# Parting joined results on VectorE instead of GpSimd, in four pieces of two operations

## The chip, the cores and the metric

The kernel runs on one core of one Trainium2 chip. The metric is device time in microseconds, from one launch to its end. The core has five engines, each with an instruction queue that it works through in order: TensorE (PE, with its weight loads as PEld), VectorE (DVE), ScalarE (ACT), GpSimd (POOL) and SyncE (SP). In this kernel SP issues all DMA transfers.

## The reference, cut to what matters

The input x has four images of 64 channels of 256x256, in fp32. Four layers follow each other. Layers 0, 2 and 3 are long convolutions with a filter for each channel (here done as products with Toeplitz matrices, along columns and rows, and a residual `x * bias`). Layer 1 goes to a Haar basis, mixes the channels twice, shrinks, adds up, and goes back:

```
f1 = haar2d(x)
acc = 0
for i in range(2):
    f3 = f1 * v[i]
    f4 = einsum('bchw,oc->bohw', f3, conv_w[i])
    acc += sign(f4) * relu(abs(f4) - tau[i])
x = haar2d(acc, inverse=True) + x
```

`haar2d` adds and subtracts neighbours, scaled by the square root of one half, over eight levels along the rows and then the columns.

## The kernel before, in words

The work is cut in three phases, each over two groups of two images (GROUPS, NB). Phase A does layer 0 and the forward Haar transform and writes coefficients (`coef`) to HBM. Phase B mixes the channels of one group and writes the results (`mixed`, and for the last group's raw second products `unshrunk`). Phase C reads them, does the inverse transform and layers 2 and 3, and writes the output.

Each phase is a list of small pieces of code. `beside` interleaves two lists by hand: phase B of group 0 lies beside the second half of phase A, phase B of group 1 beside the first part of phase C. The order in which the pieces issue is the order on every engine's queue, since the schedule is written out by hand; tiles come from pools, in rings with a fixed number of buffers by tag.

Phase B runs over 64 steps s of two units u = 2s and 2s+1 (one for each `v[i]`, `conv_w[i]`). Each unit has three pieces j = 0, 1, 2. The operations of a unit and the lines under which the profile shows them before the change:

- `mix`, TensorE, L651: eight products of 64x512 into PSUM tile f (tile ft is the input).
- `multiply`, VectorE, L670: x = f * v, into a tile of ring "x", which has two buffers. In group 1, odd units from step 2 on are raw: L667 copies the product out instead, and nothing else is done with it here.
- `sign` and `magnitude`, ScalarE, L676 and L685. Sign fills a tile of ring "m", which has three buffers. In group 0 the magnitude goes to PSUM, in group 1 in place into the x tile.
- `less` and `threshold`, VectorE, L690 and L695: subtract tau, then max with 0 and multiply by the sign.
- `exchange`, ScalarE, L701, a copy named other.
- `add`, GpSimd, L713 and L714 (even units, which start a tile of ring "gt", three buffers) and L710 (odd units).
- `store`, SP, L719: gt goes to `mixed`.
- `load_v` (L603 and L605: v and its thresholds) and `load_f` (L592: ft), SP.

Steps 0 and 1 need something more, since the rows of the coarsest Haar levels lie in their tiles. `join` (VectorE, L623 to L630) does the last level before mixing, once for each image, on 64 partitions and 256 elements at a time. `part` (GpSimd, L636 to L643) undoes it on the results gt of steps 0 and 1, on 64 partitions and 512 elements (both images). Both take a spare tile through the helper `four`. `part` is called in the piece u = 6, j = 0, right after `add(4)`, and the stores of steps 0 and 1 come right after it.

What else lies around: phase A's forward transform on GpSimd (L388, L390), its evictions of PSUM on ScalarE (L488) and VectorE (L508, L521); phase C's inverse transform on GpSimd (L429, tiles i and at the end ci), the product c0ps on TensorE (L352) that takes ci, the Toeplitz products c1r, c1c, c2r, c2c (L340), their evictions on ScalarE (L897 z, L909 ch) and VectorE (L928 cy and o), the scaling of loaded coefficients g on ScalarE (L406), and on SP the loads toep (L163), g (L806) and x (L150) and the stores of raw results (L727), of coef (L525) and of the output (L937).

Of the kernel before, what the change touches and what calls it, by code (L numbers as in the profile page):

```python
# [41 lines left out]
F32 = mybir.dt.float32  # L42
AF = mybir.ActivationFunctionType
ALU = mybir.AluOpType
# [3 lines left out]
P = 128  # L48
# [20 lines left out]
NB = B // GROUPS  # L69
# [14 lines left out]
W = 2 * N  # L84
# [16 lines left out]
def conv_haar_kernel(  # L101
    ctx: ExitStack, tc: tile.TileContext, x, zT, w1, wbd, cols, wo, decay, wo_first, decay_first, bias, forward, inverse, pack, v, tau, per_level, v_rows, out
):
    nc = tc.nc
# [16 lines left out]
    def pool(name, bufs, stack=ctx, **kw):  # L121
        return stack.enter_context(tc.tile_pool(name=name, bufs=bufs, reuse_waits="tile", **kw))
# [173 lines left out]
    def half(r):  # L296
        return slice(r * ROW, (r + 1) * ROW)
# [150 lines left out]
    def run(ops, count):  # L448
        for _ in range(count):
            next(ops, None)  # L450
# [117 lines left out]
    def phase_b(grp):  # L568
# [4 lines left out]
        def raw(u):  # L573
            return grp == GROUPS - 1 and u % 2 == 1 and FULL <= u // 2 < STEPS
# [4 lines left out]
        def step_of(ap, s, images):  # L579

            n = NB * W
            at = ap.offset + s // 2 * PAIR + s % 2 * P // CI * n
            rows = bass.AP(ap.tensor, at, [[n, P // CI], [STEPS // 2 * PAIR, CI], [1, n]])
            return rows, images.rearrange("p b w -> p (b w)")

        def load_f(s):
            if s >= STEPS:
                return
            d = st[s]
            d["f"] = bp.tile([P, NB, W], F32, tag="ft", name=f"ft_{grp}_{s}", bufs=4)  # L590
            rows, f = step_of(coef[grp], s, d["f"])
            nc.sync.dma_start(f, rows)  # L592
# [17 lines left out]
            if grp == GROUPS - 1 and not raw(2 * s + 1):  # L610
                fetch(1, 1, "raw")

        def four(name, at, b):

            tiles = [st[s][name] for s in range(2)]
            tiles.append(bp.tile([P, NB, W], F32, tag="m", name=f"spare_{name}_{grp}_{b}", bufs=3))
            return [t[at, b, bass.ts(h, N)] for t in tiles for h in range(2)]

        def join(image):

            a, b, c, d, t, u = four("f", half(image), image)
            op = nc.vector.tensor_tensor
            op(t, a, b, ALU.add)  # L623
            op(b, a, b, ALU.subtract)
            op(u, c, d, ALU.add)
            op(d, c, d, ALU.subtract)
            nc.vector.tensor_scalar(c, b, math.sqrt(2.0), None, ALU.mult)
            nc.vector.tensor_scalar(d, d, math.sqrt(2.0), None, ALU.mult)
            op(a, t, u, ALU.add)
            op(b, t, u, ALU.subtract)  # L630

        def part():

            a, b, c, d, t, u = four("g", half(0), slice(0, NB))
            op = nc.gpsimd.tensor_tensor
            op(t, a, b, ALU.add)  # L636
            op(b, a, b, ALU.subtract)
            nc.gpsimd.tensor_scalar(u, c, math.sqrt(2.0), None, ALU.mult)
            op(a, t, u, ALU.add)
            nc.gpsimd.tensor_scalar(d, d, math.sqrt(2.0), None, ALU.mult)  # L640
            op(c, b, d, ALU.add)
            op(d, b, d, ALU.subtract)
            op(b, t, u, ALU.subtract)  # L643

        def mix(u):
            s, i = divmod(u, 2)
            un[u]["f4"] = bps.tile([P, NB, W], F32, tag="f4", name=f"f4_{grp}_{u}", bufs=1)
            for b in range(NB):
                for r in range(2):
                    q = r ^ b  # L650
                    nc.tensor.matmul(  # L651
                        un[u]["f4"][half(q), b, :],
                        mixers[0][half(r), bass.ts(i, C)],
                        st[s]["f"][half(r), b],
                        start=True,
                        stop=True,
                        tile_position=(r * ROW, q * ROW),
                    )
# [5 lines left out]
        def multiply(u):  # L664
            if raw(u):
                t = st[u // 2]["raw"] = bp.tile([P, NB, W], F32, tag="raw", name=f"raw_{grp}_{u}", bufs=3)
                nc.vector.tensor_copy(t, un[u]["f4"])  # L667
                return
            un[u]["x"] = bp.tile([P, NB, W], F32, tag="x", name=f"x_{grp}_{u}", bufs=2)
            nc.vector.tensor_tensor(un[u]["x"], un[u]["f4"], both(u, "v"), ALU.mult)  # L670

        def sign(u):
            if raw(u):
                return
            un[u]["m"] = bp.tile([P, NB, W], F32, tag="m", name=f"m_{grp}_{u}", bufs=3)
            nc.scalar.activation(un[u]["m"], un[u]["x"], AF.Sign)  # L676

        def magnitude(u):
            if raw(u):
                return  # L680
            if grp == GROUPS - 1:
                un[u]["a"] = un[u]["x"]
            else:
                un[u]["a"] = bps.tile([P, NB, W], F32, tag="a", name=f"a_{grp}_{u}", bufs=1)
            nc.scalar.activation(un[u]["a"], un[u]["x"], AF.Abs)  # L685

        def less(u):
            if raw(u):
                return
            nc.vector.tensor_tensor(un[u]["a"], un[u]["a"], both(u, "tau"), ALU.subtract)  # L690

        def threshold(u):
            if raw(u):
                return
            nc.vector.scalar_tensor_tensor(un[u]["m"], un[u]["a"], 0.0, un[u]["m"], ALU.max, ALU.mult)  # L695

        def exchange(s):

            st[s]["other"] = bp.tile([P, W], F32, tag="other", name=f"other_{grp}_{s}", bufs=2)
            for q in range(2):  # L700
                nc.scalar.copy(st[s]["other"][half(q)], st[s]["f"][half(1 - q), 1])  # L701

        def add(u):
            s, i = divmod(u, 2)
            if raw(u):
                un[u].clear()
                return
            m = un[u]["m"]
            if i:
                nc.gpsimd.tensor_tensor(st[s]["g"], st[s]["g"], m, ALU.add)  # L710
            else:
                g = st[s]["g"] = bp.tile([P, NB, W], F32, tag="gt", name=f"gt_{grp}_{s}", bufs=3)
                nc.gpsimd.tensor_tensor(g[:, 0], m[:, 0], st[s]["f"][:, 0], ALU.add)  # L713
                nc.gpsimd.tensor_tensor(g[:, 1], m[:, 1], st[s]["other"], ALU.add)  # L714
            un[u].clear()

        def store(s):
            to, g = step_of(mixed[grp], s, st[s]["g"])
            nc.sync.dma_start(to, g)  # L719
            st[s].clear()  # L720

        def store_raw(s):
            if s < FULL:
                t = st[s]["raw"] = bp.tile([P, NB, W], F32, tag="raw", name=f"none_{grp}_{s}", bufs=3)
                nc.gpsimd.memset(t, 0.0)
            to, g = step_of(unshrunk, s, st[s]["raw"])
            nc.sync.dma_start(to, g)  # L727

        def piece(u, j):

            s, i = divmod(u, 2)
            if j == 0:
                if u < units:
                    multiply(u)
                if 0 < u <= units and grp == GROUPS - 1:
                    less(u - 1)
                if 1 < u <= units + 1:
                    add(u - 2)
                if i == 0 and s == 3:
                    part()  # L740
                    store(0)
                    store(1)
                if i == 0 and s > 3 and not raw(2 * s - 3):
                    store(s - 2)
                if i and raw(2 * s - 1):
                    store(s - 1)
            elif j == 1:
                if 0 < u <= units and grp < GROUPS - 1:
                    less(u - 1)
                if u + 1 < units and grp < GROUPS - 1:  # L750
                    mix(u + 1)
                if u < units:
                    sign(u)
                if i and s < STEPS and grp == GROUPS - 1:
                    store_raw(s)
                if 0 < u <= units:
                    threshold(u - 1)
                if i == 0 and s > 0:

                    load_v(s + 2)  # L760
                    if grp < GROUPS - 1:
                        load_f(s + 3)
            else:
                if u + 1 < units and grp == GROUPS - 1:
                    mix(u + 1)
                if i and s > 0 and grp == GROUPS - 1:
                    load_f(s + 3)
                if u < units:
                    magnitude(u)
                if i == 0 and s < STEPS:  # L770
                    exchange(s)

        def start():
            mixers.append(bp.tile([P, P], F32, tag="mix", name=f"mix_{grp}", bufs=1))
# [257 lines left out]
    bp = pool("b", 2, during)  # L1032
# [4 lines left out]
    a = a[-2 * A_PIECES :]  # L1037
# [7 lines left out]
    bp = pool("b2", 2, during)  # L1045
# [132 lines left out]
```

## Time and profile before

| | us |
|---|---|
| median of 3 runs (lowest to highest) | 2484.69 (2483.29 to 2487.93) |
| profiled execution, its own time | 2485.05 |
| its span, first to last instruction | 2483.2 |
| mean granted TensorE clock | 0.984 of full |
| busy: PE, PEld | 2261.3, 1863.9 |
| busy: DVE, ACT, POOL | 1775.6, 1392.2, 2080.2 |
| `part` in group 0, group 1 (start of first to end of last) | 456.83 to 467.7, 1132.1 to 1144.0 |

The busy times are averages over stages with different limits: phase B of group 0 runs from about 420 to 1000 of the span, that of group 1 from about 1090 to 1790, and the rest of phase C alone until the end. A line of the timeline or the chain begins with its time in us from the span's start.

### The profile page before, as it was taken

The page shows a single profiled execution, that of the slowest core. Times are in us where ns is not written, and L with a number is a line of the kernel's source. Part 1 is how long each engine was busy: PE and PEld are TensorE (multiplying, and loading weights), DVE is VectorE, ACT ScalarE, POOL GpSimd, SP SyncE. Part 2 cuts the span into 40 slices and gives each one's busy share as a digit, 9 for nine tenths or more (in the row PEclk, how much of TensorE's full clock was granted, in tenths as well). Part 3 has the DMA queues.
Part 4 walks back from the last instruction along what each step waited for, and adds up shares of the span by engine and source line. Part 5 has one row for each costly group of instructions (what it writes and reads, how often), then busy time and mean ns, then how long its engine had stood idle before and what let it go on. Part 6 is the DMA issues. An engine that isn't in the chain of part 4 may idle for free.

```text
span 2483.2 us, 119306 instructions
## 1 busy us (share of the span) xinstructions
PE 2261.3 (91%) x53298; PEld 1863.9 (75%) x53298; DVE 1775.6 (72%) x1943; ACT 1392.2 (56%) x2318; POOL 2080.2 (84%) x2428
## 2 busy tenths in 40 slices
PE   6999999777777777777999999999899999999999
PEld 5788887444444444555887887888899999999998
DVE  4533335799999999766777778777577777777763
ACT  1322233677777777255666766667555655565652
POOL 2988887999999999778776878778879999999990
PEclk9999999899999999988999999999999999999999
DMA  6788887699999999657998999999866666666643
GB/s 184 246 281 302 300 297 300 246 372 347 359 346 357 357 339 353 211 188 261 328 325 310 342 331 321 334 324 337 280 204 219 211 220 216 218 213 213 220 161 109
DMA packets 222968, 688.03 MB, mean 277 GB/s; under 512 B 31470, under 2 KB 32815, under 8 KB 218232
## 3 DMA queue, kind: packets, MB, share of 16 engines
q1 hardware_dynamic: 222456, 680.40, 78.1%
q8 instruction: 419, 6.86, 1.1%
q14 instruction: 93, 0.76, 0.1%
HBM read 428.16 MB, written 252.12 MB: 274 GB/s over the span
## 4 chain that ended last, share of the span: by engine, by line
PE 47%; DMA 2%; DVE 2%; issue 1%; POOL 1%; ACT 1%; SPq 0%; DVEq 0%; ACTq 0%; POOLq 0%
PE c2c L340 10%; PE c2r L340 10%; PE c1c L340 10%; PE c1r L340 9%; PE c0ps L352 4%; PE f L651 4%; DMA g<-mixed 1%; DMA toep<-filt 1%; DVE cy L928 0%; POOL i L429 0%; DVE x L670 0%; DMA unshrunk<-raw 0%; DVE x L690 0%; ACT ch L909 0%; DMA out<-o 0%
## 5 line engine op out<-in xcount | busy, mean ns | idle before, releaser
L429 POOL TENSOR_TENSOR i<-i,g 128x16 f32<-128x16 f32 x744 | 441.5, 615 | 27.2
L651 PE MATMUL f<-ft,mix 64*64 64x512 f32 x2048 | 302.8, 614 | 117.6 <-DVE x L670 104.0
L340 PEld LDWEIGHTS a2ps<-toep,ay 64*64 64x64 f32 x8192 | 298.4, 136 | 122.7 <-DVE f L521 50.8
L340 PE MATMUL a2ps<-toep,ay 64*64 64x128 f32 (+3 forms) x8192 | 336.5, 303 | 23.2 <-DVE f L521 18.1
L340 PEld LDWEIGHTS c1c<-toep,ch 64*64 64x64 f32 x8192 | 311.8, 133 | 43.8 <-issue 14.0
L340 PEld LDWEIGHTS c2c<-toep,ch 64*64 64x64 f32 x8192 | 304.8, 134 | 51.1 <-issue 12.8
L340 PEld LDWEIGHTS a1ps<-toep,x 64*64 64x64 f32 x8192 | 279.2, 134 | 65.6 <-issue 39.0
L340 PE MATMUL c1c<-toep,ch 64*64 64x128 f32 (+3 forms) x8192 | 317.2, 297 | 7.9 <-issue 4.6
L340 PE MATMUL c2c<-toep,ch 64*64 64x128 f32 (+3 forms) x8192 | 314.7, 298 | 8.5 <-ACT ch L909 7.5
L340 PE MATMUL c1r<-toep,z 64*64 64x192 f32 (+3 forms) x8192 | 317.0, 298 | 5.3 <-issue 3.2
L340 PEld LDWEIGHTS c1r<-toep,z 64*64 64x64 f32 x8192 | 298.3, 134 | 29.5 <-issue 11.9
L340 PE MATMUL a1ps<-toep,x 64*64 64x256 f32 (+3 forms) x8192 | 314.0, 299 | 6.7 <-issue 3.8
L340 PEld LDWEIGHTS c2r<-toep,cy 64*64 64x64 f32 x8192 | 298.5, 134 | 27.2 <-issue 12.5
L340 PE MATMUL c2r<-toep,cy 64*64 64x128 f32 (+3 forms) x8192 | 316.3, 298 | 2.9 <-issue 2.6
L429 POOL TENSOR_TENSOR ci<-i,g 128x1024 f32<-128x1024 f32 x124 | 313.9, 2553 | 4.5
L676 ACT ACTIVATE m<-x 128x1024 f32<-128x1024 f32 x194 | 205.9, 1061 | 158.5 <-DVE x L670 107.5
L488 ACT COPY ay<-a1ps 128x512 f32<-128x512 f32 x256 | 137.5, 589 | 272.6 <-PE a1ps L340 272.0
L713 POOL TENSOR_TENSOR gt<-m,ft 128x512 f32<-128x512 f32 x128 | 163.8, 1279 | 143.4 <-DVE m L695 136.2
L909 ACT COPY ch<-c2r 128x512 f32<-128x512 f32 x256 | 137.1, 589 | 259.7 <-PE c2r L340 259.4
L670 DVE TENSOR_TENSOR x<-f,v 128x1024 f32<-128x1024 f32 x192 | 233.4, 1216 | 29.6 <-PE f L651 26.4
L508 DVE SCALAR_TENSOR_TENSOR x<-x,bias_sb,a2ps 128x512 f32<-128x512 f32 x256 | 179.5, 742 | 94.6 <-PE a2ps L340 43.2
L909 ACT COPY ch<-c1r 128x512 f32<-128x512 f32 x256 | 137.5, 594 | 169.2 <-PE c1r L340 168.8
(86 smaller groups left out, 3983.9 us busy)
## 6 DMA issues: line engine op xcount, KB each, us to landing
toep<-filt SPq DMA_DIRECT2D x768, 112.0 KB
ft<-coef SPq DMA_DIRECT2D x128, 512.0 KB
mixed<-gt SPq DMA_DIRECT2D x128, 512.0 KB
g<-mixed SPq DMA_DIRECT2D x256, 256.0 KB
x<-in_x SPq DMA_DIRECT2D x128, 256.0 KB
coef<-f SPq DMA_DIRECT2D x128, 256.0 KB
x<-in_x SPq DMA_DIRECT2D x32, 1024.0 KB
v<-in_v SPq DMA_DIRECT2D x64, 512.0 KB
```

What stands on the lines that cost most here:

```text
L340: nc.tensor.matmul(ps[r][half(c), j % 2, k * ROW :], data[half(r), c, k, bass.ts(j, ROW)], t(r, c)[:, : N - k * ROW], start=k == 0, stop=k ...
L352: nc.tensor.matmul(ps[r][half(c)].rearrange("p h k -> p (h k)"), matrix[half(r)], pairs(r, c).rearrange("p h k -> p (h k)"), start=True, s ...
L429: engine.tensor_tensor(to, s, d, op)
L488: later(lambda y=y, ps=ps: nc.scalar.copy(y, ps))
L508: nc.vector.scalar_tensor_tensor(to, old, bias_sb[:, c : c + 1], ps, ALU.mult, ALU.add)
L651: nc.tensor.matmul(un[u]["f4"][half(q), b, :], mixers[0][half(r), bass.ts(i, C)], st[s]["f"][half(r), b], start=True, stop=True, tile_posi ...
L670: nc.vector.tensor_tensor(un[u]["x"], un[u]["f4"], both(u, "v"), ALU.mult)
L676: nc.scalar.activation(un[u]["m"], un[u]["x"], AF.Sign)
L713: nc.gpsimd.tensor_tensor(g[:, 0], m[:, 0], st[s]["f"][:, 0], ALU.add)
L909: later(lambda y=y, ps=ps: nc.scalar.copy(y, ps))
```

## The change

`part` moves from GpSimd to VectorE. It becomes a generator that gives up after each of its eight operations, and four pieces run two of them each: at the ends of the pieces (u, j) = (6, 2), (7, 0), (7, 1) and (7, 2), in both groups. The stores of steps 0 and 1 move from the piece (6, 0) to the end of the piece (7, 2). The spare tile comes from ring "x" (two buffers) instead of ring "m" (three); `join` keeps ring "m".

```diff
-        def four(name, at, b):
+        def four(name, at, b, tag, bufs):
             tiles = [st[s][name] for s in range(2)]
-            tiles.append(bp.tile([P, NB, W], F32, tag="m", name=f"spare_{name}_{grp}_{b}", bufs=3))
+            tiles.append(bp.tile([P, NB, W], F32, tag=tag, name=f"spare_{name}_{grp}_{b}", bufs=bufs))
             return [t[at, b, bass.ts(h, N)] for t in tiles for h in range(2)]
...
-            a, b, c, d, t, u = four("f", half(image), image)
+            a, b, c, d, t, u = four("f", half(image), image, "m", 3)
...
         def part():
-            a, b, c, d, t, u = four("g", half(0), slice(0, NB))
-            op = nc.gpsimd.tensor_tensor
-            op(t, a, b, ALU.add)
-            op(b, a, b, ALU.subtract)
-            nc.gpsimd.tensor_scalar(u, c, math.sqrt(2.0), None, ALU.mult)
-            op(a, t, u, ALU.add)
-            nc.gpsimd.tensor_scalar(d, d, math.sqrt(2.0), None, ALU.mult)
-            op(c, b, d, ALU.add)
-            op(d, b, d, ALU.subtract)
-            op(b, t, u, ALU.subtract)
+            a, b, c, d, t, u = four("g", half(0), slice(0, NB), "x", 2)
+            op = nc.vector.tensor_tensor
+            yield op(t, a, b, ALU.add)
+            yield op(b, a, b, ALU.subtract)
+            yield nc.vector.tensor_scalar(u, c, math.sqrt(2.0), None, ALU.mult)
+            yield op(a, t, u, ALU.add)
+            yield nc.vector.tensor_scalar(d, d, math.sqrt(2.0), None, ALU.mult)
+            yield op(c, b, d, ALU.add)
+            yield op(d, b, d, ALU.subtract)
+            yield op(b, t, u, ALU.subtract)
+
+        parted = part()
...
-                if i == 0 and s == 3:
-                    part()
-                    store(0)
-                    store(1)
...
+            at = 3 * (u - 6) + j - 2
+            if 0 <= at < 4:
+                run(parted, 2)
+            if at == 3:
+                store(0)
+                store(1)
```

## The prediction

> **What bounds the kernel now.** I read the page's busy shares first, then busy time and granted clock by stretch, then the chain of waits through the stretches where the moved work runs, then the waits of the engines and of SP's queue there, last the timeline of like operations. TensorE leads over the whole span, but the stages differ:
>
> ```profile
> PE 2261.3 (91%) x53298; PEld 1863.9 (75%) x53298; DVE 1775.6 (72%) x1943; ACT 1392.2 (56%) x2318; POOL 2080.2 (84%) x2428
> ```
>
> The stretches (start:end, length, busy us of each engine with instruction counts, granted clock, DMA share):
>
> ```profile
> 450.00:460.00 10.00, 4.13 (x56) 1.67 (x56) 5.48 (x5) 4.83 (x7) 9.77 (x10) 1.00 0.23 90
> ...
> 500.00:520.00 20.00, 16.01 (x266) 9.52 (x260) 19.21 (x19) 15.14 (x20) 18.81 (x23) 0.91 1.00 370
> ...
> 1140.00:1150.00 10.00, 0.00 (x0) 0.00 (x0) 0.00 (x0) 4.13 (x6) 9.69 (x7) 0.63 0.36 135
> ...
> 1180.00:1200.00 20.00, 20.00 (x490) 18.48 (x486) 16.14 (x17) 15.15 (x27) 15.60 (x13) 1.00 0.95 330
> ```
>
> In the mixing of group 0 (500:520) VectorE is full and sets the pace (its waits from 500 to 1000 come to 7.4 us); in that of group 1 (1180:1200) TensorE is full. In both there is a hole just after the start, with GpSimd alone busy. Group 1's hole, as the chain of waits has it (start, length, what):
>
> ```profile
> 1130.93 1.24 POOL gt L714
> 1132.17 1.23 POOL _slice(0, 2, None)_16562 L636
> ...
> 1142.74 1.26 POOL gt L643
> 1144.00 2.44 POOL i L429 x2
> ...
> 1151.21 1.11 PE c0ps L352
> ```
>
> The eight operations of `part` (L636 to L643) run from 1132.17 to 1144.00 on the path; behind them on GpSimd stand the last steps of an inverse transform (i, ci), for which TensorE waits. Waits of 440:480 (first three), 1120:1180 (next two), and of SP's queue in the two regions (engine, line, releaser: total us, times, longest):
>
> ```profile
> DVE a L690 <- ACT a L685: 10.4, 2, 6.0
> ...
> ACT m L676 <- POOL gt L643: 6.5, 1, 6.5
> ...
> DVE x L670 <- DMA v<-in_v: 1.1, 1, 1.1
> ...
> PE c0ps L352 <- POOL ci L429: 11.9, 1, 11.9
> ...
> PE c1c L340 <- ACT ch L909: 2.1, 1, 2.1
> ...
> SPq L719 <- POOL gt L643: 20.1, 1, 20.1
> ...
> SPq L719 <- POOL gt L643: 13.9, 1, 13.9
> ```
>
> In group 0 `part` runs from 456.83 to 467.7. Its spare tile sits in ring m, so ScalarE's sign waits for it, VectorE waits for ScalarE (4.41 and 5.95 us idle before two L690), and SP stands 20 us at the store of gt 0 with the loads of thresholds and v behind it: hence the later 1.1 us wait for v. In group 1 SP stands 13.9 us, and the g loads behind it land late: ScalarE reaches them at 1166.4, and TensorE waits 2.1 us for a copy behind them.
>
> [...] The last line of `join` (VectorE) with GpSimd idle, then the same line under a GpSimd ci:
>
> ```profile
> 418.44 0.41 DVE L630 TENSOR_TENSOR ft<-spare_f 64x256 f32<-64x256 f32 x1
> ...
> 1090.53 2.57 DVE L630 TENSOR_TENSOR ft<-spare_f 64x256 f32<-64x256 f32 x1
> ...
> 1090.40 2.41 POOL L429 TENSOR_TENSOR ci<-i,g 128x1024 f32<-128x1024 f32 x1
> ```
>
> The columns are start, length, engine, line, operation; 0.41 us became 2.57 [...].
>
> **The change, part by part.**
>
> 1. *GpSimd loses eight operations per group*: 10.9 us in group 0 and 11.8 in group 1 (start to end above).
>
> 2. *VectorE gains eight per group*, 64x512 each: six tensor_tensor at 0.69 and two tensor_scalar at 0.43, 5.0 us; `join`'s eight took 2.9 from first to last against 3.1 of durations, so 4.8. That is the floor. Waiting for GpSimd comes on top: group 1's two `join`s took 3.5 (a DMA wait left out) and 8.3 us instead of 2.9, that is 0.6 and 5.3 more. GpSimd is as busy where `part` will run, so I take the middle, 3 us: **8 us per group, between 4.8 and 10**. [...]
>
> 3. *Group 0.* Gone: 4.41 + 5.95 + 1.10 = 11.5 us of VectorE idle time. Paid on the same engine, which is the bound: 8 us. Net **-3.5** (-6.7 to -1.4).
>
> 4. *Group 1.* ci without `part`: 1132.2 + 2.5 (i) + 4.6 (ci) = 1139.3, just when TensorE runs dry (1139.36). But VectorE is next. c0ps also needs the PSUM pair that the second eviction of cy (L928) frees, now queued behind six operations of `part`; the mixing product after it needs x of unit 8, behind all eight. Walking VectorE's order from the end of x of unit 6 at 1130.2 at bare prices: two of part 1.3, evictions 1.4, raw 1.2, less 1.2, two of part 1.1, threshold 1.2, two of part 1.1, evictions 1.4: c0ps at about 1140, instead of 1151.2, 11 us gained. Walking again with each two-input operation waiting out one GpSimd operation (1.2 us in the additions and i, 2.3 in ci) puts the evictions' end at about 1146.7, x of unit 8 at 1149.2 and the mixing product there instead of 1152.97: 3.8 gained. GpSimd was 98% busy here, so I take the second: 3.8, plus the 2.1 us wait at 1169, which goes because the loads of g are no longer 14 us behind: **-6** (0 to -13; the ends from the two walks, and zero if something not shown steps in).
>
> 5. *DMAs.* SP issues as many as before. The four toeplitz loads, v, its thresholds and ft now pass ahead of stores 0 and 1; in group 1 so do the stores of gt 2 and raw, a g load and an ft. That costs nothing: they were what stood behind the stuck store. The stores themselves now wait for VectorE's eighth operation, and behind them on SP stand, in group 0, store 2 and the next v and ft, in group 1 the next toeplitz and three g loads. Ring gt has three tiles, so GpSimd's addition for step 3 waits until store 0 has landed. My walk issues store 0 at 466.7 (before: 467.7; addition at 472.6) and 1148 (1144.0; 1151.4). In group 1 the addition may come some us late, but GpSimd then still idles 4.39 us at 1156 to 1160 for VectorE: covered, cost 0; uncovered at most 3 us.
>
> 6. *Rings.* Ring x has two tiles and lends one: x of unit 7 in group 0 waits for the magnitude of unit 6, which ScalarE can finish at 454 when sign no longer waits: 0. In group 1 unit 7 takes no x: 0. Ring m keeps its three tiles: sign of unit 6 need not wait 5.1 us for L714; counted in 3.
>
> Sum: -3.5 - 6 = **-9.5 us** against the profiled execution's 2485.05 (span 2483.2 and 1.9 around it), 0.36 above the median of the runs, 2484.69: 2475.5. Both stages behind the holes are full on one engine, so what is gained early isn't lost again.
>
> **Rivals.**
>
> [...] Part costs 4.8 us in both groups: -6.7, then -11 - 2.1 in group 1; TensorE, less long idle, may also escape the low clock after the hole (1.99 us for eight c0ps against 1.04, and the like: up to 2.8). Together -20 to -22: **2464**. For it: `join`'s first image. Against it: GpSimd 98% busy in both windows.
>
> *The wait for the stores takes the hole's place*: the addition for step 3, and behind it the next inverse transform, come late in group 1, and only group 0's gain is left: -3, **2482**, no change that can be told. The spare tile's ring going wrong would look alike.
>
> *Slower: [...].* Place: the three stretches of VectorE in which part runs. Price: 4.8 + 8 x 1.9 (middle of 1.26 and 2.4) = 20 us in group 0 against 11.5 removed: +8.5; group 1 then gains nothing: **2493.5**. It decides from (11.5 - 4.8)/8 = 0.83 us of waiting per operation in group 0. `join`'s worst image shows 5.3/8 = 0.66, and many GpSimd operations in the window are short (0.2 to 0.6 us): against it, though not by much.
>
> **How the numbers follow.** About 5 us (0.2%) is what a measurement here can tell from no change. Forecast (-4 to -15): 0.60; [...] 0.14; stores: 0.13; slower: 0.13. A few hundredths of the first fall under 5 us and of the third over it: faster 0.72, same 0.14, slower 0.14. The range runs from the full gain to the edge of the slower case, 2462 to 2487. The likeliest case's own is 2470 to 2481.
>
> **What would show it.** Right: `part` on VectorE at 6 to 10 us per group, some operations over 1 us and beside a GpSimd one; no ScalarE wait for `part`; TensorE's wait for c0ps near 1145 under 8 us and ended by VectorE rather than ci; SP not standing over 12 us at the stores. Wrong: `part` at 0.7 us apiece throughout (the first rival); GpSimd waiting for a DMA ahead of the addition for step 3 with TensorE idle later (the second); over 1.5 us apiece (the third).

## The result, and the profile after

Run side by side, 20 executions each, the kernel before took 2488.43 us (median) and the changed one 2482.76 us (2474.07 to 2491.59). The ratio is **0.9972, 95% interval 0.9961 to 0.9982**: 4.5 to 9.7 us faster, about 7.0 (0.0028 x 2488.43). That is inside the predicted range and on the predicted side, 2 to 3 us short of the predicted 9.5. In absolute time, 2482.76 lies just above the likeliest case's own 2470 to 2481: beside it the kernel before took 3.7 us more than in the three runs that the prediction started from (2484.69).

The execution that was profiled took 2491.59 us, the slowest of the twenty, and its phase B began 2.5 us later than before's, ahead of anything that the change touches. So spans can't be compared here. I compare windows instead: the time from the start of VectorE's product x (or of the raw copy) of one unit to the start of that of a later one.

| window, us | before | after |
|---|---|---|
| group 0, unit 6 to 12 | 37.31 | 34.15 |
| group 1, unit 2 to 12 | 70.47 | 67.25 |

Together 6.4 us in the two places where `part` runs; each is one profiled execution against one. Busy time, from the page of the changed kernel:

```profile
PE 2261.5 (91%) x53298; PEld 1874.7 (75%) x53298; DVE 1792.3 (72%) x1959; ACT 1392.0 (56%) x2318; POOL 2055.6 (83%) x2412
```

The sixteen instructions (8 per group) went from POOL's count to DVE's, and TensorE's busy time stayed. The stretches of the changed kernel (start:end, length, busy us with counts of PE, PEld, DVE, ACT, POOL, granted clock, DMA share):

```profile
450.00:460.00 10.00, 5.67 (x120) 3.45 (x114) 9.71 (x11) 7.47 (x11) 9.84 (x9) 1.00 0.94 310
500.00:520.00 20.00, 14.66 (x264) 8.45 (x260) 19.57 (x20) 15.12 (x20) 18.46 (x23) 1.00 0.95 335
1140.00:1150.00 10.00, 2.54 (x8) 0.61 (x8) 9.90 (x10) 0.00 (x0) 9.86 (x10) 0.63 0.33 126
```

In 450:460 VectorE is now 97% busy where it was 55%. Over the whole window from unit 6 to 12 of group 0, the kernel before first, then the changed one, in the same columns:

```profile
449.63:486.94 37.31, 24.97 (x356) 16.23 (x360) 25.19 (x25) 19.11 (x26) 35.35 (x36) 0.82 0.53 187
```

```profile
452.60:486.75 34.15, 22.80 (x356) 15.11 (x360) 33.13 (x33) 19.35 (x26) 27.70 (x28) 0.85 0.75 248
```

VectorE's idle time there fell from 12.1 us to 1.0: the hole of group 0 is filled. In 1140:1150 VectorE has gone from 0 to 9.90 us, but TensorE only from 0 to 2.54: more than half of its hole is still there. Waits of the changed kernel's engines in 440:480 (first line) and 1120:1180 (the others), and of SP's queue in the same two stretches:

```profile
ACT m L678 <- POOL gt L716: 1.3, 1, 1.3
...
PE c0ps L352 <- DVE cy L932: 6.5, 1, 6.5
...
ACT g L406 <- DMA g<-mixed: 3.9, 2, 2.0
...
PE c1c L340 <- ACT ch L913: 0.5, 1, 0.5
...
SPq L721 <- DVE gt L643: 7.9, 1, 7.9
...
SPq L721 <- DVE gt L643: 9.2, 1, 9.2
```

No wait of ScalarE is ended by an operation of `part` any more; at 4.7 us it now waits for VectorE's x, behind it in order. TensorE's 11.9 us for ci became 6.5 us for cy: VectorE's evictions are late next. SP stands 7.9 and 9.2 us at store 0 instead of 20.1 and 13.9. The chain of waits through group 1's hole shows what stands ahead of them (start, length, what):

```profile
1138.21 2.51 DVE _slice(0, 2, None)_16631 L638
1140.75 2.71 DVE gt L639
1143.46 1.13 DVE m L697
1144.60 0.36 DVE gt L640
1144.98 0.68 DVE gt L641
1145.67 1.32 DVE cy L932 x2
1146.98 1.59 DVE gt L642
1148.60 0.69 DVE gt L643
1149.31 0.55 SPq L721
...
1155.79 0.59 SPq L810
...
1157.09 7.86 DMA g<-mixed
1164.98 0.55 ACT g L406 x3
```

`part` is still on the path, but as VectorE's work ahead of the evictions cy; behind its last operation comes store 0 (1149.31), and behind that on SP a load of g, which ScalarE receives at 1164.98.

### The profile page after: what moved, and what is told of

Read it like the earlier page. It is cut to its first block, busy times and chain, and to the rows that moved or that the text cites. A ratio compares the mean times of both kernels' runs of the same rounds, so it can differ in the third digit from the quotient of the medians.

```text
span 2489.8 us, 119298 instructions
## 1 busy us (share of the span) xinstructions
PE 2261.5 (91%) x53298; PEld 1874.7 (75%) x53298; DVE 1792.3 (72%) x1959; ACT 1392.0 (56%) x2318; POOL 2055.6 (83%) x2412
## 4 chain that ended last, share of the span: by engine, by line
PE 46%; DMA 4%; DVE 3%; issue 2%; SPq 1%; ACT 1%; DVEq 0%; ACTq 0%
PE c2r L340 10%; PE c2c L340 10%; PE c1c L340 9%; PE c1r L340 9%; PE c0ps L352 4%; PE f L653 3%; DMA g<-mixed 2%; DVE x L692 1%; DVE cy L932 1%; DMA toep<-filt 1%; SPq L163 1%; DVE x L672 0%; DMA raw<-in_v 0%; DMA unshrunk<-raw 0%; DVE m L697 0%
## 5 line engine op out<-in xcount | busy, mean ns | idle before, releaser
L429 POOL TENSOR_TENSOR i<-i,g 128x16 f32<-128x16 f32 x744 | 436.0, 606 | 27.2
L340 PEld LDWEIGHTS a2ps<-toep,ay 64*64 64x64 f32 x8192 | 303.6, 136 | 117.6 <-DVE f L521 52.7
L340 PE MATMUL a2ps<-toep,ay 64*64 64x192 f32 (+3 forms) x8192 | 337.1, 303 | 24.8 <-DVE f L521 20.5
L340 PEld LDWEIGHTS c1c<-toep,ch 64*64 64x64 f32 x8192 | 310.8, 133 | 42.6 <-issue 13.9
L340 PEld LDWEIGHTS a1ps<-toep,x 64*64 64x64 f32 x8192 | 285.5, 134 | 62.5 <-issue 39.3
L340 PE MATMUL c2c<-toep,ch 64*64 64x128 f32 (+3 forms) x8192 | 317.1, 299 | 11.9 <-ACT ch L913 10.0
L340 PE MATMUL c2r<-toep,cy 64*64 64x256 f32 (+3 forms) x8192 | 319.7, 298 | 5.1 <-issue 3.8
L340 PE MATMUL c1r<-toep,z 64*64 64x256 f32 (+3 forms) x8192 | 314.5, 297 | 5.7 <-issue 3.7
```

What stands on the lines that cost most here:

```text
L340: nc.tensor.matmul(ps[r][half(c), j % 2, k * ROW :], data[half(r), c, k, bass.ts(j, ROW)], t(r, c)[:, : N - k * ROW], start=k == 0, stop=k ...
L429: engine.tensor_tensor(to, s, d, op)
```

## Experiments

Each kernel differs from the changed one only as shown. "g0" is the window of group 0 from unit 6 to 12, "g1" that of group 1 from unit 2 to 12. Where a text on record gives units 4 to 12, g1 is longer by units 2 to 4. These took 10.6 or 12.0 us in different executions, whatever the kernel, and lie before `part` begins. With `part` on GpSimd in group 1, the kernel before took 12.03 us there and 58.44 for the rest, the change in group 0 alone 10.64 and 60.23: the time saved early was lost again later. So I start at unit 2, from where the two agree (70.47 and 70.87).

| kernel | ratio to before (95%) | g0 | g1 |
|---|---|---|---|
| before | 1 | 37.31 | 70.47 |
| the change | 0.9972 (0.9961 to 0.9982) | 34.15 | 67.25 |
| in group 0 alone | 0.9989 (0.9977 to 1.0002) | 34.47 | 70.87 |
| in group 1 alone | 0.9977 (0.9963 to 0.9991) | 36.37 | 66.90 |
| pieces left on GpSimd | 1.0001 (0.9991 to 1.0012) | 40.17 | 70.31 |
| spare tile from ring m | 0.9978 (0.9968 to 0.9987) | 37.12 | 66.86 |
| GpSimd quiet in group 0 | not compared | 31.05 | 66.93 |
| scalings on ScalarE | 0.9958 (0.9942 to 0.9974) | 32.75 | 65.17 |
| gt ring of four | 0.9959 (0.9946 to 0.9973) | 33.81 | 67.46 |
| one unit later | 0.9956 (0.9941 to 0.9970) | 35.47 | 63.08 |
| one unit later, gt ring of four | 0.9959 (0.9946 to 0.9971) | 34.06 | 61.68 |
| the same, scalings on ScalarE | 0.9946 (0.9934 to 0.9958) | 33.09 | 62.28 |

### Each group by itself

```diff
+                if i == 0 and s == 3 and grp != 0:
+                    part_before()
+                    store(0)
+                    store(1)
...
-            if 0 <= at < 4:
+            if grp == 0 and 0 <= at < 4:
...
-            if at == 3:
+            if grp == 0 and at == 3:
```

> The change in group 0 alone; group 1 parts on GpSimd as before. Measure beside the time: start of x of unit 6 to start of x of unit 12 in group 0 (37.3 us before, 34.2 after the change), and unit 4 to unit 12 in group 1 (58.4 before, 56.6 after). If each group's hole pays by itself: 34.2 in group 0, 58.4 in group 1, time about 3 us (0.13%) under the kernel before. If the whole gain sits in group 1: no change in the time, and the 3 us of group 0 lost again in the same stage (unit 127 as late as before, counted from unit 6).

> The change in group 1 alone. If each group pays by itself: 37.3 us in group 0 (units 6 to 12), 56 to 57 in group 1 (units 4 to 12), time 2 to 4 us under the kernel before; the two halves' gains add up to that of the whole change. If group 1's gain is eaten by what follows (stores, loads, low clock): no change in the time.

(`part_before` is `part` as the kernel before has it, and the second kernel swaps the two groups.) Each window follows its own group: g0 is 34.47 with the change in group 0 and 36.37 without, g1 is 70.87 without and 66.90 with. The halves' ratios, -0.11% (an interval that reaches 1) and -0.23%, add up to the whole's -0.28% within what the intervals allow. So the gain is two local ones, and neither half undoes the other; which is larger the times can't tell. Taking the executions with the same code in a group, g0 went from between 36.4 and 37.3 without the change to between 34.2 and 34.5 with it, and g1 from between 70.5 and 70.9 to between 66.9 and 67.3.

### The engine, or the schedule and the ring?

```diff
-            op = nc.vector.tensor_tensor
+            op = nc.gpsimd.tensor_tensor
...
-            yield nc.vector.tensor_scalar(u, c, math.sqrt(2.0), None, ALU.mult)
+            yield nc.gpsimd.tensor_scalar(u, c, math.sqrt(2.0), None, ALU.mult)
```

(and the other scaling in the same way)

> Ring x, the four pieces and the late stores as in the change, but the eight operations stay on GpSimd. If the engine is what counts: GpSimd, nearly as full as VectorE, still pays 11 us in group 0, so 35.5 to 38 us for units 6 to 12; in group 1 ci still stands behind part of it, TensorE waits 8 to 12 us for ci and units 4 to 12 take 57 to 60; no gain in the time, or a loss. If ring m and the stuck loads were what cost: 34 us or less in group 0, a gain of 3 us or more.

The ring, the four pieces and the late stores without the engine give nothing: 1.0001, and group 0 is 2.9 us worse than before, worse than I expected (35.5 to 38). Waits of this kernel in 440:480 (first line) and 1120:1180 (the others):

```profile
DVE x L672 <- POOL gt L643: 12.9, 1, 12.9
...
DVE x L672 <- POOL gt L643: 11.8, 1, 11.8
...
PE f L653 <- DVE x L672: 8.3, 1, 8.3
...
PE c0ps L352 <- POOL ci L429: 4.5, 1, 4.5
```

The spare tile now comes from ring x, so VectorE's product of unit 8 stands behind GpSimd's last part operation, 12.9 and 11.8 us. TensorE's wait for ci falls from 11.9 to 4.5 us, as it should with `part` spread out, and is followed by 8.3 us for x. The wait had only moved from ring m to ring x. So the tile of ring x, lent without a wait to the engine that fills that ring, was not free for another one.

```diff
-            a, b, c, d, t, u = four("g", half(0), slice(0, NB), "x", 2)
+            a, b, c, d, t, u = four("g", half(0), slice(0, NB), "m", 3)
```

> The change with the spare tile from ring m (three buffers) instead of ring x. If the ring counts: in group 0 the spare takes the buffer of unit 4's sign, which GpSimd's addition of unit 4 frees only about 4.7 us after VectorE would begin, so units 6 to 12 take 37 to 39 us instead of 34.2; group 1, whose raw units use no m, stays at 56 to 57. If the ring does not matter: 34.2 and 56.6.

Here the engine moves and the ring does not. Waits of this kernel in 440:480:

```profile
ACT m L678 <- POOL gt L712: 5.5, 2, 5.0
...
DVE g_slice(0, 2, None)_7825 L636 <- POOL gt L716: 3.5, 1, 3.5
```

VectorE's first part operation waits 3.5 us for GpSimd's addition to give back an m tile, and a later sign of ScalarE 5.0 us. Group 0 falls back to 37.12, all but 0.2 us of before. The ring without the engine lost 2.9 us, the engine without the ring gained 0.2: **in group 0 the gain needs both**, and moving the engine alone only trades one VectorE loss for another. (The ratio, 0.9978, can't be told from the change's; this rests on the window and the waits.) In group 1, where every odd unit is raw and uses neither ring, the ring makes no difference (66.86 against 66.90).

### What makes the operations of part long

`part` took 8.26 us of durations in group 0 (1.11, 0.99, 0.41, 1.64, 2.02, 0.68, 0.68, 0.73) and 11.68 in group 1 (1.32, 1.65, 2.57, 2.71, 0.42, 0.68, 1.65, 0.68). The next kernel leaves out GpSimd's work beside it in group 0: the forward transform of one tile and the additions of step 2 become fills with zeros (`quiet` is such a fill), so its output is not that of the reference.

```diff
-                s["ops"] = forward_free(s["x1"], s["fw"], f"f{t}_")
+                s["ops"] = quiet(s["fw"]) if t == 35 else forward_free(s["x1"], s["fw"], f"f{t}_")
...
+            if grp == 0 and s == 2:
+                if i == 0:
+                    st[s]["g"] = bp.tile([P, NB, W], F32, tag="gt", name=f"gt_{grp}_{s}", bufs=3)
+                    nc.gpsimd.memset(st[s]["g"], 0.0)
+                un[u].clear()
+                return
```

> The change, with GpSimd's work beside part in group 0 left out: the forward transform of tile 35 and the additions of step 2 are replaced by zero fills. It asks why part takes 8.3 us of durations in group 0 and 11.7 in group 1 when eight such operations alone would take about 5. Theory ([...]): with GpSimd nearly idle each of the eight operations falls to 0.68 us (0.42 for the scalings), 5.0 in sum, and units 6 to 12 of group 0 take 30 to 32 us instead of 34.15. Group 1, where nothing is left out, keeps 11 to 12 us. Rival (the operations are slow for another cause, such as their half-tile of 64 partitions, the in-place operands or waits inside part): 8 us in group 0 as before, and units 6 to 12 within 0.5 us of 34.15 unless less or threshold also run shorter.

The same four operations (L636, L637, L639 and L640 of the changed kernel, five lines further down in this one), VectorE's timeline, changed kernel first (start, length, engine, line, operation):

```profile
456.26 1.11 DVE L636 TENSOR_TENSOR g_slice(0, 2, None)_7825<-gt 64x512 f32<-64x512 f32 x1
457.41 0.99 DVE L637 TENSOR_TENSOR gt<-gt 64x512 f32<-64x512 f32 x1
...
459.90 1.64 DVE L639 TENSOR_TENSOR gt<-g_slice(0, 2, None)_7825 64x512 f32<-64x512 f32 x1
...
463.86 2.02 DVE L640 TENSOR_SCALAR gt<-gt 64x512 f32<-64x512 f32 x1
```

```profile
453.38 0.67 DVE L641 TENSOR_TENSOR g_slice(0, 2, None)_7811<-gt 64x512 f32<-64x512 f32 x1
454.09 0.68 DVE L642 TENSOR_TENSOR gt<-gt 64x512 f32<-64x512 f32 x1
...
456.28 0.68 DVE L644 TENSOR_TENSOR gt<-g_slice(0, 2, None)_7811 64x512 f32<-64x512 f32 x1
459.28 0.41 DVE L645 TENSOR_SCALAR gt<-gt 64x512 f32<-64x512 f32 x1
```

With GpSimd quiet each sum or difference takes 0.67 to 0.69 us, each scaling 0.41, together 4.91 us against 8.26. The scaling at 463.86 is the plainest case: it ends at 465.88, and GpSimd's addition beside it, on POOL's timeline of the changed kernel, ran until 465.60.

```profile
463.25 2.35 POOL L712 TENSOR_TENSOR gt<-gt,m 128x1024 f32<-128x1024 f32 x1
```

So the waiting for GpSimd cost 3.35 us in group 0 (8.26 - 4.91), and g0 fell by 3.1 us without it. VectorE's other operations in the window took as long as before (1.21 to 1.23 us for x, less and threshold), so the rest of the work did not get shorter. The scaling reads one tile, the sum of L639 two, and both took longer beside GpSimd: 2.02 us instead of 0.41, and 1.64 instead of 0.68.

### What a shorter part is worth

```diff
             a, b, c, d, t, u = four("g", half(0), slice(0, NB), "x", 2)
+            nc.scalar.mul(u, c, math.sqrt(2.0))
+            nc.scalar.mul(d, d, math.sqrt(2.0))
...
-            yield nc.vector.tensor_scalar(u, c, math.sqrt(2.0), None, ALU.mult)
...
-            yield nc.vector.tensor_scalar(d, d, math.sqrt(2.0), None, ALU.mult)
```

> The change with the two scalings by the square root of two moved to ScalarE, issued in the first of the four pieces; six operations stay on VectorE. In the change the scalings cost VectorE 0.41 + 2.02 us in group 0 and 2.57 + 0.42 in group 1. Theory (they cost what they last, and ScalarE has room): units 6 to 12 of group 0 at about 32 us (34.15 with the change), and in group 1 c0ps released by the evictions about 2 to 3 us earlier (144 instead of 146.5 on the clock of that stage), x of unit 8 at about 1146.5; 2 to 5 us below the change in all. Rival 1 (the next two-input operation of VectorE then waits out the GpSimd operation that the scaling waited for): part as long as before, the same time within 2 us. Rival 2 (ScalarE is late: the scalings stand before its sign and magnitude, or wait for the additions of steps 0 and 1): VectorE waits for ScalarE and the time rises by 1 to 3 us.

`part` fell to 7.5 us (1.11, 0.98, 0.67, 1.75, 2.28, 0.68) in group 0 and 7.85 in group 1. In group 0 that is only 0.8 us less: the waiting passed to the next operation in part (L642 took 2.28), as the first rival had it. g0 nevertheless fell by 1.4 us and g1 by 2.1. My expectation of an earlier c0ps failed: TensorE still waited for cy, 7.0 us. With six operations in pieces of two, all six stand ahead of the second eviction, as six of the change's eight do, and I had not counted that. The waiting also passed on, to the threshold between them. VectorE's threshold of unit 6 in the changed kernel, then in this one:

```profile
1143.39 1.21 DVE L697 SCALAR_TENSOR_TENSOR m<-x,m 128x1024 f32<-128x1024 f32 x1
```

```profile
1130.85 3.35 DVE L697 SCALAR_TENSOR_TENSOR m<-x,m 128x1024 f32<-128x1024 f32 x1
```

Of the 3.8 us by which part became shorter in group 1, 2.1 came back in this one operation. The mixing product behind c0ps, which had waited another 1.5 us for x in the change, now followed at once. The interval of the ratio (0.9942 to 0.9974) overlaps that of the change, so its gain over the change rests on the windows.

### Where part stands: before or behind the evictions

```diff
-            at = 3 * (u - 6) + j - 2
+            at = 3 * (u - 7) + j - 2
...
-                g = st[s]["g"] = bp.tile([P, NB, W], F32, tag="gt", name=f"gt_{grp}_{s}", bufs=3)
+                g = st[s]["g"] = bp.tile([P, NB, W], F32, tag="gt", name=f"gt_{grp}_{s}", bufs=4)
```

Both edits, both with the scalings on ScalarE, the second edit alone, and the first alone:

> The change with all four pieces one unit later, (7,2) to (8,2), the stores of steps 0 and 1 with the last of them, and ring gt of four tiles instead of three so that the addition of step 3 has not to wait for store 0. Theory (in group 1 the second eviction of cy stands behind six operations of part, and c0ps behind it): with part behind the evictions, c0ps comes at 1140 to 1142 instead of 1146.5, TensorE's clock does not fall to 0.63, and units 4 to 12 of group 1 take 50 to 54 us instead of 56.60; group 0 the same within 1 us; 3 to 7 us below the change. Rival (part costs VectorE the same 11 us a little later, and the mixing product after c0ps waits for x instead): units 4 to 12 within 1.5 us of 56.60 and the time within 2 us of the change.

> The two edits together: pieces one unit later with ring gt of four, and the two scalings on ScalarE. If both theories hold, group 0 about 32 us for units 6 to 12 and group 1 49 to 52 us for units 4 to 12, 5 to 10 us below the change. [...], the same as the later pieces alone, within 1.5 us.

> The change with ring gt of four tiles instead of three, nothing else: the addition of step 3 no longer waits until store 0 has landed (1.2 us of GpSimd waiting in group 1 with the change). It asks whether the later stores cost anything. Theory (the wait is covered, as the prediction costed it at zero): the windows of both groups within 0.5 us of the change's (34.15 in group 0, 56.3 to 56.6 in group 1) and the time within 2 us of it. Rival (the late store holds back GpSimd and, behind the addition, the next inverse transform): units 4 to 12 of group 1 shorter by 1 to 3 us.

> The change with all four pieces and the stores one unit later, (7,2) to (8,2), and ring gt left at three tiles. It parts the two edits made together before (later pieces, and a fourth gt tile), which took units 4 to 12 of group 1 to 51.0 us and the time to 0.9959 of the kernel before. Theory (the place of the pieces does it, since c0ps then has no part operation ahead of its evictions): units 4 to 12 of group 1 at 51 to 53 us. But the addition of step 3 stands on GpSimd in the piece (8, 0), ahead of the stores in (8, 2), and waits for store 0 to land, with the end of the inverse transform behind it. If that wait decides, c0ps waits for ci again, the window goes back to 56 us or more, and group 0 loses 2 us or more as well: then it was the fourth tile that made the later place usable.

The place does it. One unit later, g1 falls from 67 to 63.08 and, with the fourth gt tile, 61.68. The fourth tile alone moves neither window by over 0.4 us from the profiled change (33.81, 67.46), so the late stores cost at most that in the change. Its ratio, 0.9959, overlaps the change's, and I read no gain into it. The ratio of the later pieces alone, 0.9956, overlaps it too; there the windows show the gain.

The texts on record take it that the addition of step 3 waits for store 0. GpSimd's timeline of the changed kernel shows that only in group 0 (first line below; the stores were issued from 468.10 on). In group 1 the addition ran at 1144.98, 4.3 us before store 0 was issued at 1149.31; the store of gt 2, issued at 1135.87, had probably given its tile back by then.

```profile
471.25 1.27 POOL L715 TENSOR_TENSOR gt<-m,ft 128x512 f32<-128x512 f32 x1 [3.72 <-DVE x L672]
...
1144.98 1.81 POOL L715 TENSOR_TENSOR gt<-m,ft 128x512 f32<-128x512 f32 x1
...
1173.20 1.28 POOL L715 TENSOR_TENSOR gt<-m,ft 128x512 f32<-128x512 f32 x1 [1.16 <-DMA mixed<-gt]
```

The third line, a wait of 1.2 us that the profile puts down to a store, belongs to step 5, and the kernel before and the one with four gt tiles have the same 1.16 us there, ended by VectorE's threshold: it has nothing to do with the late stores. In group 0 the fourth tile did take the 3.72 us away (the addition of step 3 then ran without idle time before it), and the window gained 0.3.

TensorE's timeline with the later pieces, ring gt at three tiles and then at four (start, length, operation, idle time before and what ended it):

```profile
1136.01 1.09 PE L352 MATMUL c0ps<-ci,inverse_sb 64*64 64x512 f32 x8 [1.97 <-POOL ci L429]
1138.41 1.99 PE L653 MATMUL f<-ft,mix 64*64 64x512 f32 x8 [1.31 <-DVE x L672]
1140.17 6.50 PE L340 MATMUL c2c<-toep,ch 64*64 64x256 f32 x128
```

```profile
1136.38 1.09 PE L352 MATMUL c0ps<-ci,inverse_sb 64*64 64x512 f32 x8 [1.94 <-POOL ci L429]
1138.77 1.09 PE L653 MATMUL f<-ft,mix 64*64 64x512 f32 x8 [1.31 <-DVE x L672]
1139.68 4.54 PE L340 MATMUL c2c<-toep,ch 64*64 64x256 f32 x128
```

TensorE waits 2 us where it waited 6.5, and for ci again: the evictions are no longer last. So it was part's operations ahead of them that made the rest of the hole. At the later place they also waited less for GpSimd in group 1, 6.9 us of durations instead of 11.7; how much of the gain that adds is not separated here. In group 0 the later place gains nothing (34.06, 35.47): VectorE has the same operations either way, and with three gt tiles part took 9.9 us there.

These two also bear on a side question. After an idle time of 1.97 us the clock of the one fell, and its c2c took 6.50 us instead of 4.54; after 1.94 us that of the other did not. (In 1140:1145 the granted clock was 0.58 in the first and 1.00 in the second. Both had another 1.31 us of idle time behind c0ps.) What decides between the two is not shown here. From unit 4 to 12 both took 51.0 us all the same (51.05 and 51.01). TensorE waited 1.5 us for ch in the first and 3.0 in the second, which also waited 0.9 us for VectorE: what the low clock lost, shorter waits gave back.

The last of them, later pieces with four gt tiles and ScalarE's scalings, has the lowest ratio: 0.9946 (0.9934 to 0.9958), 10.5 to 16.4 us below the kernel before, and its interval lies clear of the change's (0.9961 to 0.9982). It beats both the kernel before and the change, on five executions. It is not told apart from the later pieces without the scalings (0.9959, 0.9946 to 0.9971).

## Why the prediction was right, and where not

1. *GpSimd loses eight operations a group.* Right (its busy time fell by 24.6 us in all). Beside VectorE's work its own operations got longer, though: in group 1 the two i and the two ci ahead of c0ps took 3.97 and 5.70 us, and 2.48 and 4.64 before, with VectorE idle. What that is worth hangs on the terms below.

2. *VectorE pays 8 us per group, between 4.8 and 10.* The floor was right: 4.91 us measured with GpSimd quiet, 0.67 to 0.69 us for each sum or difference and 0.41 for each scaling. (The 0.69 and 0.43 that it counted with are not shown by the trace of the kernel before. There `join`'s 256 elements took 0.41 to 0.42 us in a sum or difference and 0.28 in a scaling with GpSimd idle, and the scalings of 128x512 at L220 0.44 us.) In group 0 8.26 us of durations fits the 8. In group 1 they came to 11.68 us, over the upper end: the bound was taken from `join`'s worst image, where three of the eight operations took over 1.3 us (1.35, 1.48, 2.57), and in `part` five did. This term was too small by 3.7 us there. It cost nothing against the forecast, because the walk in step 4 already had it, by an estimate of mine: each two-input operation waits out one GpSimd operation, 1.2 or 2.3 us long in the trace before. (Measured in group 1: four of the six took 1.32 to 2.71 us, two 0.68.)

3. *Group 0: -3.5.* Measured -3.16 in the profiled windows, -1.9 to -3.2 over the executions with the same code. The sum is the one forecast: 11.5 us of idle time gone, 8.26 paid. The mechanism is as argued from ScalarE's sign: with the engine moved and ring m kept, the gain is gone.

4. *Group 1: -6.* The first term, 3.8 us, had the right path and nearly the right size. Counted from the end of x of unit 6 (1130.2 before, 1130.8 after), c0ps was walked to 16.5 us and came after 15.6, waiting for VectorE; the mixing product behind x of unit 8 was walked to 19.0 and came after 19.6, 3.1 us sooner than in the kernel before. Over the executions with the same code g1 fell by 3.2 to 4.0 us. **The term that failed is the other one, 2.1 us** for TensorE's wait for a copy behind late loads of g. The step said that these loads "are no longer 14 us behind". They still were behind store 0, as step 5 itself lists, and the end of SP's wait moved from 1144.0 to 1149.3. Counted from x of unit 2, the g that ScalarE waits for came at 61.30 us before (1166.42 - 1105.12) and at 57.87 after (1164.98 - 1107.11): 3.4 us earlier, which is about what g1 gained (3.2) and no more. The kernel before (its chain, then its VectorE timeline), and the changed one:

```profile
1160.27 6.12 DMA g<-mixed
...
1166.42 0.03 ACT g L406
...
1105.12 1.22 DVE L670 TENSOR_TENSOR x<-f,v 128x1024 f32<-128x1024 f32 x1 [1.38 <-PE f L651]
```

```profile
1107.11 1.23 DVE L672 TENSOR_TENSOR x<-f,v 128x1024 f32<-128x1024 f32 x1 [1.38 <-PE f L653]
```

ScalarE's wait for it hardly changed (2.2 and 2.0 us), and neither did what follows it. TensorE's wait did fall from 2.1 to 0.5 us, but because TensorE itself lost time on the way: c2c took 6.55 us instead of 5.34, at a granted clock of 0.68 instead of 0.84, and 1.1 us of new idle time stood in c2r. A wait that shrinks because the waiter is late is no gain. The change in group 0 alone shows the same from the other side: there group 1 is as before, its c0ps came 1.4 us sooner after x of unit 2, g came at 61.33 all the same, and TensorE waited 4.3 us for the copy. With the pieces and stores one unit later, the next toeplitz loads and one of the three g loads passed ahead of store 0 (1134.80 and 1137.66, store 0 at 1143.04), and g came at 52.6.

5. *DMAs at zero.* Right in size for the stores: they issued at 468.1 and 1149.3 (walked: 466.7 and 1148), and a fourth gt tile took at most 0.3 us off a window. The reason given fits group 0 alone, where GpSimd idled 3.72 us before the addition for step 3; in group 1 this addition did not wait for store 0 at all. The loads of g behind store 0 are the failed term of step 4.

6. *Rings at zero.* Right: VectorE both fills ring x and uses the spare, and no wait for a ring x tile shows. With GpSimd using it the same loan cost VectorE 12.9 and 11.8 us of waiting.

The sum without the failed term is -3.5 - 3.8 = -7.3 us; measured -7.0 (-4.5 to -9.7). That it meets the number so closely is partly luck, with an interval 5 us wide and 6.4 us in the two profiled windows. Of the rivals, the first (2464, `part` at 4.8 us in both groups) is refuted by quiet GpSimd: the waiting cost 3.35 us in group 0, and in group 1 11.68 - 4.91 = 6.8 us. Its extra gain from an undisturbed clock was worth nothing in the pair shown above. The store wait as a new hole is refuted by group 1's addition for step 3, which ran before the store, and by the fourth tile in group 0. The slower case priced an operation's waiting at 1.9 us as the middle of 1.26 and 2.4, which is 1.83, and set 0.83 us per operation as the point where it decides; group 0 showed 3.35/8 = 0.42, group 1 (11.68 - 4.91)/8 = 0.85. By its own sum it would have come true with group 1's waiting in group 0, so the distance from it was smaller than its 0.13 suggests.

Not settled: how much of the later pieces' gain in g1 between three and four gt tiles (63.08 and 61.68) is the tile. Units 2 to 4 alone differ by 1.4 us there, and from unit 4 on they agree, so there is no sign of it. Nor is it settled whether anything that the windows gain or lose comes back in the hundreds of microseconds behind them; only the ratios speak for that.

## What to carry to other kernels

When work moves to another engine, look at what stands behind it in that engine's order and where its scratch tile comes from: here the ring decided whether the move paid in one group, and six operations ahead of an eviction limited it in the other, where a place one unit later shortened the window by another 4 to 6 us. Two waits in a row on a path aren't two gains: before adding the second, check that its cause (here a store on SP's queue) comes earlier, not only that the wait is listed. And price work on VectorE beside a busy GpSimd from both ends, bare and with every operation waiting one out, since it came to between 1.7 and 2.4 times the bare price in the change, and to 1.4 times at the later place in group 1.

## What was not expected of the hardware

- A scaling of 64x512 on VectorE, 0.41 us by itself, took 2.02 and 2.57 us beside a GpSimd operation: the longest of all eight in proportion, though it reads only one tile.
- The low TensorE clock (c2c 6.50 us instead of 4.54) came after an idle time of 1.97 us and stayed away after 1.94, and left the windows from unit 4 to 12 equal.
